# The convolution's edge columns: copied by VectorE beside its taps, and by POOL once per block; the first block's normalisation in two halves

## The chip, the cores and the metric

The kernel runs on one core of a Trainium2 chip. The core has five engines that work side by side, each on its own queue and in that queue's order: TensorE (PE in the profile) multiplies matrices, VectorE (DVE), ScalarE (ACT) and GpSimd (POOL) work on elements, and SyncE (SP) issues transfers. They wait for one another through semaphores. The metric is the time of one execution on the device in microseconds.

## The reference

The program is two layers on 2 sequences of 4,096 tokens with 512 channels, all in float32. What follows is the part that matters here, the first layer's opening:

```python
xn = _layernorm(x, axis=-1)
x1 = xn @ w1_w.T + w1_b
x_conv = _silu(_depthwise_conv(x1, conv_w))   # 3 taps along the sequence, zeros beyond its ends
v = _silu(xn @ v1_w.T + v1_b)
x_ssm = _ssm(x_conv, A, B_ssm, C_ssm, D_ssm)  # a linear recurrence over the sequence
attn = x_ssm * v @ w2_w.T + w2_b
ffn  = quantised(xn) @ quantised(weight).T + bias   # a six-bit grid, one scale to 32 elements
x = x + attn + ffn
```

The second layer (linear attention with 16 heads, and a gated feed-forward part) takes this x. Depthwise convolution means that each channel is filtered by itself: output t of a channel is w0·x1[t−1] + w1·x1[t] + w2·x1[t+1].

## The kernel before

The 8,192 tokens are cut into 16 blocks (NK) of 512 tokens (T), eight to a sequence (NB); 512 channels make four groups (CC) of 128. The kernel has stages one after another: the first, from the start to 472.7 us, is the one that the change is in. The later ones are the recurrence, the mixing with the quantised product, and the second layer. Within a stage a scheduler orders the instructions of each engine by the order of the program and its own estimates; what is written first is not always issued first.

The first stage loops over the blocks n. One turn of it does this:

- `projected(n)` (line 339) has TensorE make eight products of 128 channels by 512 tokens, each from four matrix multiplications (line 154). The first four, with the weight w1, give x1, the convolution's input; the other four, with v1, give v. Products go to four PSUM banks in turn (`acc`), so a product has to wait until the bank that was used four products earlier has been emptied. ScalarE empties them: line 351 adds the bias and writes x1, line 366 takes the silu and writes v, which a transfer sends to memory (line 367).
- The block's x1 is a tile of 514 columns for each channel group: column 0 is the last token of the block before, columns 1 to 512 are its own tokens, and column 513 is the first token of the next block. After each group's eviction `halo` (line 329) fills the edges. On POOL it copies column 512 of the block before into column 0 (line 334), and the own first token, column 1, into column 513 of the block before (line 335). At the ends of a sequence it writes zeros (lines 332 and 337).
- `tapped(n − 1, o)` (line 394) filters channel group o of the block before, which is now complete: tap 0 on ScalarE (line 397, columns 0 to 511), taps 1 and 2 on VectorE (line 399, columns from 1 and from 2). The silu on ScalarE (line 406), the transposition on VectorE (line 408) and the transfer cd on SP (line 409) are held back until the next group's eviction has been written down, by the list `tapping`.
- `turned(n + 1)` (line 320) prepares the next block's input, xnT, with channels on the partitions: sixteen rescalings of 128x128 on ScalarE (line 128) and four transpositions on VectorE (line 324). It needs each token's scale and bias.
- `measured` (line 293) makes these for two blocks at a time, in every second turn: bn_stats and bn_aggr on VectorE (lines 123 and 124), then `rstd` (line 105), a chain of small operations: VectorE (line 108), a square root on ScalarE (line 110), and VectorE again (lines 112 to 116, and 140 for the bias). `spread_out` moves the numbers through memory to another layout (SP, lines 132 and 134).
- Beside this, single tiles are quantised for the later product (ScalarE line 128, VectorE lines 176 to 193 and 389, POOL lines 180 and 194; the same for the weight with line 376), loaded on SP (xq, line 381), and the tables of the recurrence are made (VectorE lines 221 to 266, POOL lines 216, 232, 241).

SP issues, in its own order, the loads of x for the statistics (line 290), of the inputs to be turned (xi, line 317) and of xq, and the stores cd. A transfer that waits for its data holds back all transfers behind it.

The first block is different, because nothing can be loaded ahead of it. `first_turned` (line 299) waits for the statistics of all four tiles of 128 tokens, scales the four tiles on VectorE (line 304), and TensorE transposes them against the identity (line 148), with copies out of PSUM on ScalarE (line 149). The statistics of all four tiles come from one call of `measured(0, ...)`.

ScalarE computes silu and square root from different tables; where it goes from one to the other, the profile shows an ACT_TABLE_LOAD of 1.28 us under the line that needs it.

Of the kernel before, what the change touches and what calls it, by code (L numbers as in the profile page):

```python
# [10 lines left out]
F32 = mybir.dt.float32  # L11
I32 = mybir.dt.int32
AF = mybir.ActivationFunctionType
ALU = mybir.AluOpType
# [29 lines left out]
def block_kernel(ctx: ExitStack, tc: tile.TileContext, a: dict, out: bass.AP):  # L44
# [57 lines left out]
    def window(ap, steps):  # L102
        return bass.AP(tensor=ap.tensor, offset=ap.offset, ap=[list(ap.ap[0])] + steps)

    def rstd(out_ap, var_ap, n):

        v = small.tile([P, n], F32, tag="rs_v", name="rs_v")
        nc.vector.tensor_scalar(v, var_ap, EPS_LN, None, ALU.add)  # L108
        s = small.tile([P, n], F32, tag="rs_s", name="rs_s")
        nc.scalar.activation(s, v, AF.Sqrt)  # L110
        r = small.tile([P, n], F32, tag="rs_r", name="rs_r")
        nc.vector.reciprocal(r, s)
        e = small.tile([P, n], F32, tag="rs_e", name="rs_e")
        nc.vector.tensor_tensor(e, v, r, ALU.mult)
        nc.vector.scalar_tensor_tensor(e, e, -0.5, r, ALU.mult, ALU.mult)
        nc.vector.scalar_tensor_tensor(out_ap, e, 1.5, r, ALU.add, ALU.mult)

    def layernorm_stats(xt, mv):

        n = mv.shape[1]  # L120
        st = small.tile([P, n, 6], F32, tag="st", name="st")
        for j in range(n):
            nc.vector.bn_stats(st[:, j, :], xt(j))
            nc.vector.bn_aggr(mv[:, j, :], st[:, j, :])
        rstd(mv[:, :, 1], mv[:, :, 1], n)

    def rescaled(dst, src, mv):
        nc.scalar.activation(dst, src, AF.Identity, bias=mv[:, 0:1], scale=mv[:, 1:2])  # L128
# [9 lines left out]
    def as_scale_and_bias(mv):  # L138

        nc.vector.scalar_tensor_tensor(  # L140
            mv[:, :, 0], mv[:, :, 0], -1.0, mv[:, :, 1], ALU.mult, ALU.mult
        )
# [150 lines left out]
    def measured(n, xts):  # L293

        mv = mv0[:, n : n + len(xts) // TJ].rearrange("p n j k -> p (n j) k")
        layernorm_stats(lambda j: xts[j], mv)
        as_scale_and_bias(mv)

    def first_turned(work, xts):

        xnT = work.tile([P, CC, T], F32, tag="xnT", name="xnT")
        xn = work.tile([P, TJ, D], F32, tag="xi", name="xn")
        for j in range(TJ):
            nc.vector.tensor_scalar(
                xn[:, j, :], xts[j], mv0[:, 0, j, 1:2], mv0[:, 0, j, 0:1], ALU.mult, ALU.add
            )
        for j in range(TJ):
            transposed(xnT[:, :, j * P : (j + 1) * P], xn[:, j, :], ("tr", "mm")[j % 2])
        return xnT
# [16 lines left out]
            )  # L326
        return xnT

    def halo(n, o, x1, before):

        if n % NB == 0:
            nc.gpsimd.memset(x1[:, o, 0:1], 0.0)
        else:
            nc.gpsimd.tensor_copy(x1[:, o, 0:1], before[:, o, T : T + 1])
            nc.gpsimd.tensor_copy(before[:, o, T + 1 : T + 2], x1[:, o, 1:2])  # L335
        if n % NB == NB - 1:
            nc.gpsimd.memset(x1[:, o, T + 1 : T + 2], 0.0)

    def projected(work, n, xnT, before):

        x1 = work.tile([P, CC, T + 2], F32, tag="x1", name="x1")
        tapping = []

        def finish():
# [3 lines left out]
        for o in range(CC):  # L348
            pm = acc()
            product(pm, lambda k: w1[:, k, o * P : (o + 1) * P], lambda k: xnT[:, k, :])  # L350
            nc.scalar.activation(x1[:, o, 1 : T + 1], pm, AF.Identity, bias=w1_b[:, o, :])  # L351
            halo(n, o, x1, before)

            finish()
            if n:
                tapping.append(tapped(work, n - 1, before, o))
            if n == NK - 1 and o:

                tapping.append(tapped(work, n, x1, o - 1))
# [642 lines left out]
    with tc.tile_pool(name="tab", bufs=1) as tab:  # L1002
# [3 lines left out]
        with pool("a", 2) as work, pool("pm", 1) as pm:  # L1006
# [5 lines left out]
            v1 = load_weight("v1_w")  # L1012
            v1_b, conv_w = column("v1_b"), column("conv_w", 3)
            xi = laid(work, 1)
            measured(0, xts[0])
            xnT = first_turned(work, xts.pop(0))
            xts[1] = fetched(work, 1)
            measured(1, xts.pop(1))
# [190 lines left out]
```

## Time and profile before

| what | value |
| --- | --- |
| time, median of 3 runs | 2396.13 us (2393.2 to 2397.08) |
| the profiled execution: time | 2395.06 us |
| the profiled execution: span | 2393.3 us |
| TensorE busy | 2356.1 us, 98% |
| VectorE busy | 1530.0 us, 64% |
| ScalarE busy | 1013.0 us, 42% |
| POOL busy | 478.0 us, 20% |
| first product of the first stage | at 14.01 us |
| end of the first stage's products | at 472.7 us |
| 56 copies at line 335, duration | median 186 ns, up to 1179 ns |

The span is the time from the first to the last instruction that the profiler saw; the execution's own time is 1.8 us longer. A row of a timeline gives the start of a group of instructions, its length, engine, line, operation, the tile written and the tiles read, and how many they were; in square brackets stands how long the engine had been idle, and which instruction ended that idle time. A row of the waits gives the waiting instruction, the one it waited for, the sum in us, how many times, and the longest. A row of a table by stretches gives the busy time of each engine in that stretch, the granted clock of TensorE as a share of the full one (PEclk), the share of the transfer engines, and the rate of transfers.

### The profile page before, as it was taken

The page shows a single profiled execution, that of the slowest core. Times are in us where ns is not written, and L with a number is a line of the kernel's source. Part 1 is how long each engine was busy: PE and PEld are TensorE (multiplying, and loading weights), DVE is VectorE, ACT ScalarE, POOL GpSimd, SP SyncE. Part 2 cuts the span into 40 slices and gives each one's busy share as a digit, 9 for nine tenths or more (in the row PEclk, how much of TensorE's full clock was granted, in tenths as well). Part 3 has the DMA queues.
Part 4 walks back from the last instruction along what each step waited for, and adds up shares of the span by engine and source line. Part 5 has one row for each costly group of instructions (what it writes and reads, how often), then busy time and mean ns, then how long its engine had stood idle before and what let it go on. Part 6 is the DMA issues. An engine that isn't in the chain of part 4 may idle for free.

```text
span 2393.3 us, 21964 instructions
## 1 busy us (share of the span) xinstructions
PE 2356.1 (98%) x6400; PEld 1104.6 (46%) x6400; DVE 1530.0 (64%) x3050; ACT 1013.0 (42%) x1929; POOL 478.0 (20%) x534
## 2 busy tenths in 40 slices
PE   8999999999999999999999999999999999999999
PEld 3433444466444444444444555444444444445554
DVE  6888764554576654267769778666552265557777
ACT  5875674344233333146663222233333236652222
POOL 0121210122243332100102112233332100001111
PEclk9999999999999999999999999999999999999999
DMA  7854432467833342212265445433432212264331
GB/s 255 304 131 141 140 141 92 138 208 273 304 115 110 114 120 84 66 35 97 93 228 185 144 138 195 157 110 115 120 106 75 62 39 81 93 215 141 129 132 57
DMA packets 253832, 328.12 MB, mean 137 GB/s; under 512 B 55952, under 2 KB 117392, under 8 KB 252688
## 3 DMA queue, kind: packets, MB, share of 16 engines
q1 hardware_dynamic: 224624, 259.59, 34.2%
q10 hardware_dynamic: 29088, 67.12, 7.2%
q8 instruction: 51, 0.84, 0.2%
q14 instruction: 69, 0.57, 0.1%
HBM read 205.38 MB, written 121.27 MB: 136 GB/s over the span
## 4 chain that ended last, share of the span: by engine, by line
PE 67%; DVE 4%; DMA 1%; ACT 1%; issue 1%; POOL 1%; SPq 0%; POOLq 0%; ACTq 0%; DVEq 0%
PE p_acc L154 18%; PE p_tr L154 9%; PE p_acc L698 8%; PE p_mm L667 7%; PE p_mm L652 7%; PE p_mm L823 6%; PE p_acc L823 6%; PE p_tr L823 2%; PE p_mm L950 1%; PE p_tr L950 1%; PE p_acc L652 1%; PE p_tr L652 1%; PE p_acc L667 1%; PE p_acc L488 0%; DVE t L886 0%
## 5 line engine op out<-in xcount | busy, mean ns | idle before, releaser
L154 PE MATMUL p_acc<-xnT,w_v_w 128*128 128x512 f32 x512 | 227.8, 600 | 10.3 <-ACT x L351 10.3
L698 PE MATMUL p_acc<-k,x 128*128 128x512 f32 x512 | 229.9, 592 | 0.9 <-ACT k L733 0.9
L154 PE MATMUL p_acc<-xnT,w_w_w 128*128 128x512 f32 x512 | 223.1, 593 | 2.7 <-DVE xnT L324 1.1
L154 PE MATMUL p_acc<-w_W_v,t 128*128 128x512 f32 x512 | 222.3, 592 | 0.0
L154 PE MATMUL p_acc<-w_W_r,xnT 128*128 128x512 f32 x448 | 201.4, 592 | 0.0
L154 PE MATMUL p_tr<-w_Wk,xnT 128*128 128x512 f32 x448 | 199.2, 592 | 0.1
L971 POOL TENSOR_TENSOR x<-x,row_beta 128x512 f32<-128x512 f32 x64 | 83.8, 1310 | 552.8 <-ACT xn L128 547.4
L667 PE MATMUL p_mm<-w_w_w,t 128*128 128x512 f32 x416 | 186.7, 592 | 0.0
L652 PE MATMUL p_mm<-w_d,t 128*128 128x512 f32 x384 | 173.6, 593 | 1.4 <-DVE x L675 1.2
L110 ACT ACTIVATE rs_s<-rs_v 128x4 f32<-128x4 f32 (+1 forms) x41 | 8.3, 205 | 391.5 <-DVE rs_v L108 391.5
L154 PEld LDWEIGHTS p_acc<-xnT,w_v_w 128*128 128x128 f32 x512 | 97.7, 192 | 137.9 <-issue 115.0
L696 POOL TENSOR_TENSOR ksum<-ksum,k 128x512 f32<-128x512 f32 x62 | 83.4, 1344 | 368.8 <-ACT k L733 368.8
L154 PEld LDWEIGHTS p_acc<-xnT,w_w_w 128*128 128x128 f32 x512 | 96.8, 190 | 126.8 <-issue 117.0
L698 PEld LDWEIGHTS p_acc<-k,x 128*128 128x128 f32 x512 | 97.2, 190 | 123.7 <-issue 120.8
L154 PEld LDWEIGHTS p_acc<-w_W_v,t 128*128 128x128 f32 x512 | 97.3, 190 | 122.5 <-issue 119.1
L732 DVE TENSOR_TENSOR k<-p_tr,row_bk 128x512 f32<-128x512 f32 x64 | 43.8, 684 | 162.1 <-PE p_tr L154 162.1
L977 ACT ACTIVATE r<-p_acc 128x512 f32<-128x512 f32 x64 | 38.2, 597 | 249.8 <-PE p_acc L154 237.5
L399 DVE SCALAR_TENSOR_TENSOR xc<-x,col_conv_w,xc 128x512 f32<-128x512 f32 x128 | 95.7, 763 | 63.1 <-POOL x L335 30.9
L154 PEld LDWEIGHTS p_tr<-w_Wk,xnT 128*128 128x128 f32 x448 | 85.0, 190 | 107.6 <-issue 104.0
L180 POOL TENSOR_TENSOR xq<-xq,mx_rs 128x512 f32<-128x512 f32 x64 | 76.4, 1194 | 269.8 <-DVE mx_rs L179 188.6
L733 ACT ACTIVATE k<-k 128x512 f32<-128x512 f32 x64 | 40.1, 627 | 203.4 <-DVE k L732 194.8
L667 PEld LDWEIGHTS p_mm<-w_w_w,t 128*128 128x128 f32 x416 | 79.0, 190 | 99.5 <-issue 99.5
(223 smaller groups left out, 4054.4 us busy)
## 6 DMA issues: line engine op xcount, KB each, us to landing
x<-in_x SPq DMA_DIRECT2D x126, 256.0 KB, 3.5
xq<-in_xi SPq DMA_DIRECT2D x64, 256.0 KB, 4.5
vd<-v ACTq DMA_DIRECT2D x64, 256.0 KB, 2.3
cd<-xs SPq DMA_DIRECT2D x64, 256.0 KB, 2.0
xg<-cd SPq DMA_DIRECT2D x16, 1024.0 KB, 6.7
v<-vd SPq DMA_DIRECT2D x64, 256.0 KB, 4.8
xd<-x SPq DMA_DIRECT2D x64, 256.0 KB, 2.0
qd<-q ACTq DMA_DIRECT2D x64, 256.0 KB, 2.0
```

The costliest lines, as they stand in the source:

```text
L154: nc.tensor.matmul(out_ap, lhsT=lhsT(k), rhs=rhs(k), start=(k == 0), stop=(k == CC - 1))
L180: nc.gpsimd.tensor_tensor(by_block(y), by_block(y), rs.unsqueeze(2).to_broadcast([P, NQ, QB]), ALU.mult)
L399: nc.vector.scalar_tensor_tensor(xc, x1[:, cc, tap : tap + T], conv_w[:, cc, tap : tap + 1], xc, ALU.mult, ALU.add,)
L652: nc.tensor.matmul(po, lhsT=xds[i][j][:, k, :], rhs=wd[:, k, :], start=(k == 0), stop=False)
L667: nc.tensor.matmul(po, lhsT=z[:, k, j * P : (j + 1) * P], rhs=w2[:, k, :], start=False, stop=(k == CC - 1),)
L696: nc.gpsimd.tensor_tensor(ksum, ksum, kt, ALU.add)
L698: nc.tensor.matmul(pg[c], lhsT=xn[:, c * P : (c + 1) * P], rhs=kt, start=first, stop=last)
L732: nc.vector.tensor_tensor(kt, pk, bk, ALU.add)
L733: nc.scalar.activation(kt, kt, AF.Relu)
L823: nc.tensor.matmul(banks[c], lhsT=lhsT(k, c), rhs=rhs(k), start=first and k == 0, stop=k == 1, skip_group_check=True,)
L950: nc.tensor.matmul(pc[:, c, :], lhsT=qT[:, 2 * c2 + c, tj], rhs=kvx[:, 2 * c2 + c, :], start=True, stop=True,)
L971: nc.gpsimd.tensor_tensor(xt[j], xt[j], beta, ALU.add)
```

## The change

The edges of the convolution are filled in another way. `halo` is gone. `from_last`, called once at the start of a block, copies column 0 of all four groups in one POOL instruction (128x4) from the block before, or writes zeros. `to_last`, called after each group's eviction where `halo` was, copies the own first column into column 513 of the block before, on VectorE instead of POOL. The zeros at a sequence's end are written for four groups at once.

The first block's statistics and scaling are done by halves, two tiles of 128 tokens each: `first_turned` itself calls `layernorm_stats` for the first two tiles and scales them on ScalarE (`rescaled`), then for the other two and scales these on VectorE as before. The second half's statistics use the place of the first half's scratch tile, which `rstd` and `layernorm_stats` now take as arguments.

```diff
@@ -102,7 +102,7 @@
     def window(ap, steps):
         return bass.AP(tensor=ap.tensor, offset=ap.offset, ap=[list(ap.ap[0])] + steps)
 
-    def rstd(out_ap, var_ap, n):
+    def rstd(out_ap, var_ap, n, e=None):
 
         v = small.tile([P, n], F32, tag="rs_v", name="rs_v")
         nc.vector.tensor_scalar(v, var_ap, EPS_LN, None, ALU.add)
@@ -110,19 +110,21 @@
         nc.scalar.activation(s, v, AF.Sqrt)
         r = small.tile([P, n], F32, tag="rs_r", name="rs_r")
         nc.vector.reciprocal(r, s)
-        e = small.tile([P, n], F32, tag="rs_e", name="rs_e")
+        if e is None:
+            e = small.tile([P, n], F32, tag="rs_e", name="rs_e")
         nc.vector.tensor_tensor(e, v, r, ALU.mult)
         nc.vector.scalar_tensor_tensor(e, e, -0.5, r, ALU.mult, ALU.mult)
         nc.vector.scalar_tensor_tensor(out_ap, e, 1.5, r, ALU.add, ALU.mult)
 
-    def layernorm_stats(xt, mv):
+    def layernorm_stats(xt, mv, st=None, e=None):
 
         n = mv.shape[1]
-        st = small.tile([P, n, 6], F32, tag="st", name="st")
+        if st is None:
+            st = small.tile([P, n, 6], F32, tag="st", name="st")
         for j in range(n):
             nc.vector.bn_stats(st[:, j, :], xt(j))
             nc.vector.bn_aggr(mv[:, j, :], st[:, j, :])
-        rstd(mv[:, :, 1], mv[:, :, 1], n)
+        rstd(mv[:, :, 1], mv[:, :, 1], n, e)
 
     def rescaled(dst, src, mv):
         nc.scalar.activation(dst, src, AF.Identity, bias=mv[:, 0:1], scale=mv[:, 1:2])
@@ -300,10 +302,24 @@
 
         xnT = work.tile([P, CC, T], F32, tag="xnT", name="xnT")
         xn = work.tile([P, TJ, D], F32, tag="xi", name="xn")
-        for j in range(TJ):
-            nc.vector.tensor_scalar(
-                xn[:, j, :], xts[j], mv0[:, 0, j, 1:2], mv0[:, 0, j, 0:1], ALU.mult, ALU.add
-            )
+        for half in range(2):
+            js = range(2 * half, 2 * half + 2)
+            mv = mv0[:, 0, 2 * half : 2 * half + 2]
+
+            if half:
+                layernorm_stats(lambda j: xts[2 + j], mv, st=place)
+            else:
+                place = small.tile([P, 2, 6], F32, tag="st", name="st")
+                layernorm_stats(lambda j: xts[j], mv, e=place[:, 0, 0:2])
+            as_scale_and_bias(mv)
+            for j in js:
+                if half:
+                    nc.vector.tensor_scalar(
+                        xn[:, j, :], xts[j], mv0[:, 0, j, 1:2], mv0[:, 0, j, 0:1],
+                        ALU.mult, ALU.add,
+                    )
+                else:
+                    rescaled(xn[:, j, :], xts[j], mv0[:, 0, j, :])
         for j in range(TJ):
             transposed(xnT[:, :, j * P : (j + 1) * P], xn[:, j, :], ("tr", "mm")[j % 2])
         return xnT
@@ -326,19 +342,23 @@
             )
         return xnT
 
-    def halo(n, o, x1, before):
-
+
+    def from_last(n, x1, before):
         if n % NB == 0:
-            nc.gpsimd.memset(x1[:, o, 0:1], 0.0)
+            nc.gpsimd.memset(x1[:, :, 0:1], 0.0)
         else:
-            nc.gpsimd.tensor_copy(x1[:, o, 0:1], before[:, o, T : T + 1])
-            nc.gpsimd.tensor_copy(before[:, o, T + 1 : T + 2], x1[:, o, 1:2])
+            nc.gpsimd.tensor_copy(x1[:, :, 0:1], before[:, :, T : T + 1])
         if n % NB == NB - 1:
-            nc.gpsimd.memset(x1[:, o, T + 1 : T + 2], 0.0)
+            nc.gpsimd.memset(x1[:, :, T + 1 : T + 2], 0.0)
+
+    def to_last(n, o, x1, before):
+        if n % NB:
+            nc.vector.tensor_copy(before[:, o, T + 1 : T + 2], x1[:, o, 1:2])
 
     def projected(work, n, xnT, before):
 
         x1 = work.tile([P, CC, T + 2], F32, tag="x1", name="x1")
+        from_last(n, x1, before)
         tapping = []
 
         def finish():
@@ -349,7 +369,7 @@
             pm = acc()
             product(pm, lambda k: w1[:, k, o * P : (o + 1) * P], lambda k: xnT[:, k, :])
             nc.scalar.activation(x1[:, o, 1 : T + 1], pm, AF.Identity, bias=w1_b[:, o, :])
-            halo(n, o, x1, before)
+            to_last(n, o, x1, before)
 
             finish()
             if n:
@@ -1012,7 +1032,6 @@
             v1 = load_weight("v1_w")
             v1_b, conv_w = column("v1_b"), column("conv_w", 3)
             xi = laid(work, 1)
-            measured(0, xts[0])
             xnT = first_turned(work, xts.pop(0))
             xts[1] = fetched(work, 1)
             measured(1, xts.pop(1))
```

## The prediction

> **What bounds the kernel now.** I read the page's busy line first, then TensorE's waits, then stretches of the first stage, then the timeline around the longest stall.
>
> ```profile
> PE 2356.1 (98%) x6400; PEld 1104.6 (46%) x6400; DVE 1530.0 (64%) x3050; ACT 1013.0 (42%) x1929; POOL 478.0 (20%) x534
> ```
> ```profile
> PE p_acc L154 <- ACT x L351: 10.3, 8, 3.4
> PE p_tr L148 <- DVE xn L304: 9.7, 1, 9.7
> ...
> PE p_acc L154 <- DVE xnT L324: 1.1, 1, 1.1
> ```
> ```profile
> core 0: us, PE busy (x) PEld busy (x) DVE busy (x) ACT busy (x) POOL busy (x), PEclk, DMA share, GB/s
> ...
> 156.30:181.00 24.70, 21.13 (x48) 8.95 (x48) 20.00 (x33) 17.89 (x39) 9.36 (x5) 0.99 0.44 94
> 181.00:187.50 6.50, 6.31 (x8) 2.70 (x9) 6.50 (x8) 6.25 (x10) 0.18 (x1) 0.51 0.37 113
> ...
> 335.30:472.70 137.40, 137.39 (x320) 60.91 (x321) 68.76 (x89) 68.26 (x120) 9.69 (x41) 1.00 0.33 114
> ```
> ```profile
> 175.94 1.88 PE L154 MATMUL p_acc<-xnT,w_v_w 128*128 128x512 f32 x4
> 181.19 6.33 PE L154 MATMUL p_acc<-xnT,w_v_w 128*128 128x512 f32 x7 [3.37 <-ACT x L351]
> ```
> ```profile
> 174.00 3.62 DVE L237 TENSOR_TENSOR kf<-kf,col_D_ssm 128x4 f32<-128x4 f32 x1
> ...
> 178.80 0.74 DVE L399 SCALAR_TENSOR_TENSOR xc<-x,col_conv_w,xc 128x512 f32<-128x512 f32 x1
> ```
> ```profile
> 179.57 0.63 ACT L406 ACTIVATE xc<-xc 128x512 f32<-128x512 f32 x1 [4.82 <-DVE xc L399]
> 180.11 0.44 ACT L240 COPY kr<-kf 128x32 f32<-128x32 f32 x3
> 180.46 0.68 ACT L351 ACTIVATE x<-p_acc,col_w_b 128x512 f32<-128x512 f32 x1
> ```
>
> TensorE is busy 98% of the span, so only its own waits can be won, and the change touches only the first stage, 14.0 to 472.7 us. A block there that waits for nothing takes 27.47 us, measured over blocks 11 to 15 (137.4 / 5, give or take their edges). Sixteen make 439.5 of 458.7 us: 19.2 us are lost, and 14.0 us pass before the first product. The waits say who is late: ScalarE empties a bank (L351) too late. Its queue is in order, and a silu (L406) ahead of the eviction waits for VectorE's tap (L399). At 174 us that tap stands behind L237, four columns, which takes 3.62 us while POOL's L241 runs from 173.51 to 177.59. The eviction starts at 180.46, TensorE idles 3.37 us, and then runs at a granted 0.51 for 6.5 us: another 3.2 us. Two shorter waits in block 6 (1.84 and 2.10 us, behind evictions at 209.67 and 215.47) left the clock at 1.00. The rest: 1.06 us at block 1, 1.42 in block 3, 0.44 in block 4, 0.80 before block 5's long gap, 1.16 in block 10.
>
> **The change part by part.** The profiled execution took 2395.06 us, a span of 2393.3; it is 1.07 under the median of 2396.13. The sum is made against 2395.06.
>
> *Column copies.* Off POOL go 56 copies L334 and 56 L335 (median 186 ns for L335) and 16 memsets of about 98 ns; on come 14 copies of 128x4 and 4 memsets: some 17 us of POOL queue fall away. POOL is 20% busy, so by itself that is worth nothing. VectorE gets 56 copies of one column. No such copy is in the trace: above, L217's copy of 64 columns, 194 ns (10.9 us in all); below, the 0.07 us by which small operations follow one another at 110.02, 110.09 and 110.18 us (3.9 us in all). I take 0.1, 5.6 us, since these copies stand in a full queue like the latter. Blocks 11 to 15 (VectorE 50% busy there) and block 7 to 9 hide theirs; without that cover they cost the whole 5.6. The 20 of blocks 2 to 6 fall where VectorE is busy 84.4 of 95 us (128 to 223): 2.0 us, within 1.4 to 3.9.
>
> What VectorE gains is the wait at L399 for POOL's L335: 30.9 us in 13 waits, but 14.3 of it is one wait in the last block and most others are in blocks where TensorE sets the pace. Only 0.50 us at 319.49 in block 10 stands ahead of a late eviction, where L335 queued on POOL behind row_w_b (L1089): gain 0.5, up to 1.2 if the following waits of that block vanish with it, 0 if ScalarE is late anyway. The eviction L351 loses its wait for POOL's reads and the tap 0 (L397) gets a wait for the new block copy. That copy waits for the last eviction of the block before, ready a whole half block earlier, and for taps of two blocks back; behind it on POOL are only quantisation's L180 and L194.
>
> [...]
>
> *Order.* The order of instructions before and after differs far more than the edit: within the first stage VectorE, ScalarE, POOL and SP are reshuffled, TensorE and all later stages are not. What I find in it:
> - Block 1: the statistics' multiplier (L108) comes behind more work, and the last two of sixteen rescalings L128 behind the last silu v(0,3), which TensorE releases at 41.7. The last transposition L324 then ends near 44.0 instead of 42.8: +1.2 us (0 to 1.5, by L366 0.69, two L128 0.86, L324 0.68). Blocks 3 to 6 wait for ScalarE by the clock and swallow this; it is charged as 0 in the sum.
> - Block 2: on SP the load xq is issued after the third cd, at about 91.2, not after the fourth at 94.46. ScalarE waited 3.31 us for that load at 100.33 with sixteen rescalings behind. Gain 3.3 for the chain of ScalarE and VectorE, 0 if SP's x loads (14 ahead, up to 12.47 us) take it back.
> - Block 5: the same L237 stands behind the same L241 and costs 3.62 again; between L237 and the tap at 178.80 an L192 (0.60 to the next) and two small operations replace L188 and L176: equal within 0.2. Block 5's fourth eviction (186.25) now stands ahead of a table load (1.28) and a silu, and on the way to block 6 L376 (0.71, after 0.26 of waiting) is put off: gain 0.8 there.
>
> So the evictions of blocks 5 and 6 come 3.3 − 2.0 + 0.8 = 2.1 us earlier on one count; adding the waits of L115 and L188 behind POOL at 199.32 and 200.34 (1.01 and 1.25 us instead of the usual 0.17 and 0.41), of which the order after may spare one, I get 2.9. I take 2.9, within −4.8 (all of it, and the copies at 1.4) and +1.5 (no xq gain, and the copies at 3.9 less the 0.8, half of it swallowed by VectorE's idle 10.6 us).
>
> What is late next is block 6. TensorE now reaches it with block 3 and 4's 1.86 and most of block 5's 3.37 + 3.2 in hand, while the evictions it needs are only 2.9 earlier: its first wait grows from 1.84 to about 5 us. By the nearest row, 3.37 us of idle gave half clock and 2.10 did not, so I charge the half clock there again: 3.2 at most, less the 2.10 of the second wait, that the slower products fill: +1.1. Sum: start 0, blocks 1 to 6 −2.9 + 1.1 = −1.8, block 10 −0.8 (between 0.5 and 1.2), later 0: −2.6, 2392.5; a further −0.5 for evictions freed of POOL's wait in block 4 and 6 (between 0 and 1), 2392.0.
>
> [...]
>
> *First block's halves.* TensorE waits 9.7 us for xn (L304), begins at 9.69 and turns a tile each 0.86 us; the first product starts at 14.01. The first half's L108 comes at about 6.65 instead of 7.42, after three L123 instead of four; 0.44 to L112 and 0.97 for the small chain (7.86 to 8.99, less the mask's reductions between) give 8.06. But its two scalings go to ScalarE at 0.80 us each (the 128x512 form of L128; 0.70 with the usual overlap), and the second half's square root stands behind them, at 9.46; with 0.24 to L112, 0.97 again and 0.54 for L304 the third tile is ready near 11.2, and TensorE turned it at 11.42. Within −0.5 (all four earlier) and +0.5: taken as 0.
>
> **Rivals.**
> 1. *Large gain:* no half clock anywhere, and the chain 4.8 earlier: −4.8, block 10 −1.2, evictions −1, start −0.5, and of block 1 to 4's waits 1 more: 8.5, 2386.6. For it: the earlier xq. Against: L237 still waits for L241. All 19.2 gone would be 2375.9.
> 2. *Nothing:* the wait for POOL becomes one for ScalarE, and the x loads on SP take back the xq: 2395, within 1.5.
> 3. *Slower:* VectorE is nearly full to 223 us; the 20 added copies at 0.19 (3.8 us), with no xq gain and 0.8 spared, push the evictions of blocks 5 and 6 back by 3.0, and both first gaps pass 3.37 us, so a second half clock of 3.2 follows: +6.2, 2401.3. It decides from the point where the copies cost more than the xq brings: at 0.19 us each with a gain under 1.4. Against: the 0.07 spacing.
>
> **How the numbers follow.** Forecast (−2 to −6 counts as one case) 38%, large gain 27%, nothing 12%, slower 23%. A measurement of this kernel tells about 0.2%, 4.8 us, from no change: faster is under 2391.3, slower over 2400.9. Of the forecast case 14 fall under 2391.3 and 24 between; with the large gain 41% faster; with "nothing" 36% the same; 23% slower. The range 2383 to 2402 leaves out the far end of the large gain and of slower, some 8 and 10%. The predicted time is 2392.0; the forecast case's own range is 2389 to 2394.
>
> **What would show it.** Right: the gap at block 5's third eviction under 2 us at full clock, block 6's first gap over 3.4 us with a clock near 0.5 behind it; xq's wait at 100 us gone; first product at 14.0 ± 0.5; VectorE's copies spaced by about 0.1; block 1 begins near 44. Wrong: a copy that holds VectorE 0.2 us or more, block 5's gap as before or longer, the first product over 0.5 earlier or later, or a changed stretch after 472.7 us less its start.

## The result: slower by 0.28%

The changed kernel takes 2403.33 us (median of 7 runs, 2402.14 to 2406.6), the kernel before 2397.35 (median of 7, 2393.2 to 2399.69). The ratio is 1.0028, with a 95% interval of 1.0016 to 1.0040: slower by more than the 0.2% that can be told from no change, and above the predicted range. The profiled execution after took 2402.45 us, its span is 2400.7, which is 7.4 more than before's 2393.3.

The page's busy line of the kernel after:

```profile
PE 2359.0 (98%) x6400; PEld 1106.2 (46%) x6400; DVE 1536.9 (64%) x3110; ACT 1013.6 (42%) x1932; POOL 457.8 (19%) x424
```

POOL has lost 20.2 us of work, VectorE has gained 6.9. TensorE's own work has grown by 2.9 us with the same 6400 matmuls: some of them ran slower (block 1's first 32, below, took 16.81 us instead of 14.00). TensorE's waits after, each with the sum, the times and the longest:

```profile
PE p_acc L156 <- ACT x L371: 10.7, 5, 4.6
PE p_tr L150 <- ACT xn L130: 9.1, 1, 9.1
PE p_acc L156 <- DVE mv L126: 6.3, 1, 6.3
```

The waits for evictions (L371, before L351) are as long in sum as before, in five pieces instead of eight. The third row is new, one wait of 6.3 us. Timeline of TensorE after, three stretches:

```profile
47.66 16.81 PE L156 MATMUL p_acc<-xnT,w_w_w 128*128 128x512 f32 x32 [6.28 <-DVE mv L126]
...
188.43 9.54 PE L156 MATMUL p_acc<-xnT,w_v_w 128*128 128x512 f32 x16 [4.55 <-ACT x L371]
...
219.00 13.04 PE L156 MATMUL p_acc<-xnT,w_v_w 128*128 128x512 f32 x24 [3.87 <-ACT x L371]
```

The new wait is at the start of block 1, and the 32 matmuls behind it take 16.81 us where before they took 14.00:

```profile
42.80 14.00 PE L154 MATMUL p_acc<-xnT,w_w_w 128*128 128x512 f32 x32 [1.06 <-DVE xnT L324]
```

Blocks 5 and 6 wait 4.55 and 3.87 us, before 3.37 and 1.84 (with a second wait of 2.10 in block 6). Three stretches after, block 5, block 6 and blocks 11 to 15:

```profile
162.70:197.80 35.10, 30.50 (x66) 12.94 (x65) 29.09 (x42) 25.19 (x50) 9.74 (x5) 0.90 0.38 95
197.80:231.90 34.10, 30.23 (x66) 12.94 (x65) 29.93 (x56) 16.81 (x33) 7.45 (x8) 0.90 0.36 114
342.80:480.20 137.40, 137.40 (x322) 60.84 (x321) 70.92 (x109) 67.62 (x120) 3.37 (x6) 1.00 0.33 116
```

The granted clock falls to a mean of 0.90 in both blocks now; before, block 6 kept its clock (1.00 from 191.22 to 223.40). The last five blocks take 137.40 us as before. The first stage's products end at 480.16 us instead of 472.74: these 7.42 us are the whole difference, and the later stages are unchanged.

The clearest view of where time goes is the start of each block's first product, read off TensorE's timeline. The table has these starts as us later than in the kernel before (whose own starts stand in the second column); the other columns are kernels of the experiments below.

| block | before, at | after | halves_only | halves_turn | conv_ordered | last_dve | last_dve2 | late_tables |
| --- | --- | --- | --- | --- | --- | --- | --- | --- |
| 0 | 14.01 | −0.37 | 0.24 | 0.08 | −0.17 | 0.06 | 0.06 | −0.27 |
| 1 | 42.80 | 4.86 | 6.01 | 0.70 | 1.48 | 4.11 | 1.50 | 0.69 |
| 2 | 70.37 | 7.67 | 7.56 | 1.99 | 1.48 | 4.11 | 1.49 | 2.38 |
| 4 | 127.55 | 5.44 | 5.48 | 4.21 | 0.34 | 4.11 | 4.35 | 0.14 |
| 5 | 156.30 | 6.39 | 9.12 | 6.05 | 1.29 | 5.05 | 5.83 | 0.36 |
| 6 | 191.22 | 6.58 | 9.41 | 5.01 | 1.04 | 4.67 | 6.71 | −6.52 |
| 7 | 223.40 | 8.48 | 8.03 | 4.66 | 3.00 | 6.33 | 9.47 | −4.18 |
| 9 | 278.44 | 8.37 | 8.03 | 4.66 | 3.00 | 6.33 | 9.47 | −0.90 |
| 10 | 305.90 | 8.38 | 8.36 | 4.67 | 6.75 | 7.90 | 12.84 | −0.89 |
| 11 | 335.31 | 7.51 | 8.22 | 3.23 | 7.05 | 8.63 | 13.29 | −2.84 |

Down the column "after": −0.37 at the start, +5.23 ahead of block 1, +2.81 in block 1 (slow matmuls), −2.23 in block 3, whose short waits are gone because TensorE comes later, +1.14 in blocks 4 and 5, +1.90 in block 6, −0.1 to block 10, −0.87 in block 10. The prediction had put the loss at block 1 at 1.2 and had let it be swallowed.

One caution for reading single profiles: the part up to block 1 differs by 2 to 4 us between executions of the same instructions (see the last section), so a column is to be read from its block 1 or 2 on, and totals from the timed runs.

**What happens ahead of block 1.** VectorE's timeline after, the end of block 1's turn:

```profile
38.77 0.69 DVE L125 BATCH_NORM_STATS2 st<-x 128x6 f32<-128x512 f32 x1 [2.41 <-DMA x<-in_x]
...
43.82 0.68 DVE L340 STREAM_TRANSPOSE xnT<-xi 128x512 f32<-128x512 f32 x1
44.43 1.25 DVE L125 BATCH_NORM_STATS2 st<-x 128x6 f32<-128x512 f32 x2
45.59 0.17 DVE L126 BATCH_NORM_AGGREGATE mv<-st 128x2 f32<-128x6 f32 x1
45.67 0.66 DVE L125 BATCH_NORM_STATS2 st<-x 128x6 f32<-128x512 f32 x1
46.24 0.17 DVE L126 BATCH_NORM_AGGREGATE mv<-st 128x2 f32<-128x6 f32 x1
46.33 0.66 DVE L125 BATCH_NORM_STATS2 st<-x 128x6 f32<-128x512 f32 x1
46.90 0.70 DVE L340 STREAM_TRANSPOSE xnT<-xi 128x512 f32<-128x512 f32 x1
```

and ScalarE's last rescaling for it:

```profile
43.42 0.49 ACT L130 ACTIVATE xi<-xi,mvi 128x128 f32<-128x128 f32 x1 [0.93 <-DMA x<-in_x]
```

The last of block 1's four transpositions needs only this rescaling, done at 43.91. It starts at 46.90, because four bn_stats of later blocks, with their aggregations, stand ahead of it: 2.5 us. (The row of TensorE's wait names L126, which ended just before TensorE started; the input that it lacked is this transposition, which ends at 47.60.) Right behind the rescaling the transposition would have ended at some 44.6 us, an estimate from its own 0.7 us. So of the 4.86 us by which block 1 starts later, 1.9 are ScalarE's, whose last rescaling comes later, and 3.0 are the order of VectorE's queue. The bn_stats that waits 2.41 us for its load of x is not new: before, one waited 2.47 us in the same place, between the first two transpositions. In VectorE's order 16, 19, 21 and 25 bn_stats precede the four transpositions; before it was 15, 17, 20 and 22. The diff does not touch these lines; the scheduler put them so when the first block's statistics became two smaller sets. TensorE's clock after this wait, in steps of 2 us:

```profile
47.66:49.66 2.00, 2.00 (x3) 0.97 (x4) 2.00 (x10) 0.21 (x1) 0.00 (x0) 0.50 0.41 142
49.66:51.66 2.00, 2.00 (x4) 0.87 (x3) 2.00 (x12) 0.00 (x0) 0.26 (x1) 0.50 1.03 365
51.66:53.66 2.00, 2.00 (x4) 0.76 (x3) 0.73 (x2) 0.00 (x0) 0.79 (x1) 0.58 0.68 195
53.66:55.66 2.00, 2.00 (x6) 0.87 (x5) 0.73 (x4) 1.44 (x2) 0.00 (x0) 1.00 0.49 171
```

It is granted 0.50 for some 5.7 us behind 6.28 us of idling. The view counts 3 or 4 matmuls that touch a stretch of 2 us at half clock, and 6 in the one at full clock.

### The profile page after: what moved, and what is told of

Same layout as the page of the kernel before. It is cut to its first block, busy times and chain, and to the rows that moved or that the text cites. A ratio compares the mean times of both kernels' runs of the same rounds, so it can differ in the third digit from the quotient of the medians.

```text
span 2400.7 us, 21882 instructions
## 1 busy us (share of the span) xinstructions
PE 2359.0 (98%) x6400; PEld 1106.2 (46%) x6400; DVE 1536.9 (64%) x3110; ACT 1013.6 (42%) x1932; POOL 457.8 (19%) x424
## 4 chain that ended last, share of the span: by engine, by line
PE 69%; DVE 4%; ACT 1%; issue 1%; DMA 1%; POOL 1%; SPq 0%; POOLq 0%; ACTq 0%; DVEq 0%
PE p_acc L156 18%; PE p_tr L156 9%; PE p_acc L718 9%; PE p_mm L687 7%; PE p_mm L672 7%; PE p_mm L843 6%; PE p_acc L843 6%; PE p_tr L843 2%; PE p_mm L970 1%; PE p_tr L970 1%; PE p_acc L672 1%; PE p_acc L508 1%; PE p_acc L687 1%; PE p_acc L518 1%; PE p_tr L672 1%
## 5 line engine op out<-in xcount | busy, mean ns | idle before, releaser
L110 ACT ACTIVATE rs_s<-rs_v 128x4 f32<-128x4 f32 (+2 forms) x42 | 8.5, 205 | 391.8 <-DVE rs_v L108 391.8
L130 ACT ACTIVATE xq<-xq,mvi 128x128 f32<-128x128 f32 x256 | 104.7, 480 | 38.6 <-DMA xq<-in_xi 35.3
```

## The experiments

Two theories stood at the start: the delay at block 1, that is, the place that the scheduler gave statistics and transpositions (called A in the expectations), and the copies on VectorE's queue (B). A third came with the second set: not the edit's work but the reshuffled order of everything else. Ratios below are to the kernel before, timed beside each set, with 95% intervals.

### Each half of the change alone

conv_only has the edges copied as in the change (block copy on POOL, last column on VectorE) and the first block as before. halves_only has the first block by halves, and `halo` as before.

> The kernel before with the column copies of the change alone; the first block as before. Theory A (the halves reorder block 1, and that is the whole loss): the four transpositions of block 1 stand behind 15, 17, 20 and 22 bn_stats as in the kernel before, block 1 begins at 42.8 +- 0.5, and the time is that of before, 2397, within 4 us. Theory B (the 56 copies on VectorE push the evictions of blocks 5 and 6 back): the time is 5 to 7 us over before, with the first product at 14.0 and block 1 at 42.8, and the loss comes after 97 us.

> The kernel before with the first block by halves alone; the edge columns by POOL as before. Theory A: the transpositions of block 1 stand behind 16, 19, 21 and 25 bn_stats, as with the whole change; block 1 begins near 47.7 after an idle TensorE of some 6 us and at half clock, and the time is 5 to 9 us over before. Theory B: the time is that of before within 3 us, since the delay of block 1 is taken up by the waits of blocks 3 to 6.

Measured: conv_only 2402.5, 1.0022 (1.0013 to 1.0031); halves_only 2404.38, 1.0030 (1.0019 to 1.0042). Each part alone costs what the whole does, and the two do not add. In halves_only TensorE waits at the same place, and the same four bn_stats stand ahead of the last transposition:

```profile
48.81 15.55 PE L156 MATMUL p_acc<-xnT,w_w_w 128*128 128x512 f32 x32 [5.06 <-DVE mv L126]
```

conv_only has the bn_stats as before (15, 17, 20, 22) and no such wait. So there are two causes.

### The place of block 1 in the queues

Two edits of the whole change. stats_after holds the statistics of blocks 4 and 5 behind block 1's last transposition; turn_first lets the whole of block 1's turn go ahead of other work.

```diff
-                    xnT = turned(work, n + 1, xi)
+                    if n == 0:
+                        with tc.high_priority():
+                            xnT = turned(work, n + 1, xi)
+                    else:
+                        xnT = turned(work, n + 1, xi)
...
+                if n == 2:
+                    with tc.issue_after(turned_1[0]):
+                        measured(n + 2, xts.pop(n + 2) + xts.pop(n + 3))
```

(The first five lines are turn_first, the last three stats_after.)

> The whole change, with the statistics of blocks 4 and 5 put behind the last transposition of block 1 in VectorE's order, and nothing else asked for. Theory A (the queue on VectorE is what makes block 1 late): the last transposition follows ScalarE's last rescaling (43.9 with the whole change) at once, block 1 begins at 44.5 or earlier, a gap of 3 us instead of 6.3, without half clock; the time is 5 to 7 us below the whole change's 2403.3. Rival (the rescalings on ScalarE and their late scale and bias are what makes it late): block 1 begins within 1 us of 47.7 and the time stays above 2401.

> The whole change, with all of block 1's sixteen rescalings and four transpositions ahead of the rest, on ScalarE ahead of the silus of v and on VectorE ahead of the statistics of blocks 4 and 5. Theory A: sixteen rescalings from 29.6 at 0.39 us end near 36, the last transposition near 37, so TensorE goes from block 0 to block 1 without a gap at about 41.4; the time is 7 to 10 us below the whole change, 2394 to 2396. Rival (the loss lies in the copies and comes back in blocks 5 and 6): block 1 begins at 41.4, but the time stays above 2400.

Measured: stats_after 2403.59, 1.0032 (1.0021 to 1.0043); turn_first 2398.82, 1.0004 (0.9996 to 1.0013). In stats_after block 1's wait falls to 2.42 us, as meant, but block 4 then waits 4.39 us for an eviction, with slow matmuls behind it (10 in 7.26 us, where before 10 took 4.46), and nothing is won: A's forecast of the total failed there. In turn_first block 1 starts at 43.38 without a wait, the four transpositions having 16, 16, 16 and 17 bn_stats ahead, and the ratio falls from the whole change's 1.0028 to 1.0004. That is between the two forecasts, 2394 to 2396 and over 2400, so A's forecast of the total was too low here as well.

halves_turn is the same edit on halves_only:

> The halves alone (edge columns on POOL as before), in the scheduler's order but with block 1's rescalings and transpositions first. If the 7.5 us of the halves-alone run are block 1's place in the queues: 5 us or more below it, within 3 us of before. If the halves cost elsewhere too: above 2400.5.

Measured: 2397.07, 0.9995 (0.9986 to 1.0004), against 1.0030 without the edit. So all that the halves cost is block 1's place in the queues: with it mended they cost nothing.

### Work or order

For these the first stage's instructions are held, on each engine's queue, in the order of another kernel. The edit is a list of positions for each engine, and an order edge without a semaphore from each instruction to the next:

```diff
+        for e, order in ORDER.items():
+            for i, j in zip(order, order[1:]):
+                tc.add_manual_dep(
+                    lists[e][j], lists[e][i].name,
+                    mybir.DependencyInfo(mybir.DependencyClass.NoSync, mybir.DependencyReason.DATA),
+                    reason="order",
+                )
```

conv_ordered, halves_ordered and both_ordered have the work of conv_only, of halves_only and of the whole change in the order of the kernel before (what is new stands beside what it replaces); before_reshuffled has the work of before in the order of conv_only on VectorE, ScalarE and SP; POOL, with all its copies, is left to the scheduler. In the three ordered kernels each copy on VectorE stands directly ahead of the tap that reads it.

> The column copies of the change alone, but with the first stage's instructions held in the kernel before's order on VectorE, ScalarE, SP and POOL; each of the 56 copies stands just ahead of the tap 2 that reads it. Order theory (the copies cost next to nothing, the new order costs the 5.6 us of the copies-alone run): the time is that of before, 2397, within 2.5 us, block 1 begins at 42.8 but for the clock of the first products. Copy theory (VectorE's copies lengthen the chain): the time is 4 to 7 us over before.

> The halves alone, in the kernel before's order but for the first block's own statistics and scaling. Order theory: block 1 begins at about 42.8, not 48, and the time is that of before within 2.5 us, perhaps 0.3 less for a first product at 13.7 to 14.3. Rival (the statistics of block 1 themselves come later, whatever the order): block 1 begins after 45 and the time is 4 us or more over before.

> The whole change in the kernel before's order. Order theory: within 3 us of before, so 5 to 8 us under the whole change as the scheduler orders it; a gain over before of 0.5 to 1.5 us could come from block 10's wait for POOL. Rival: over 2401.

> The kernel before with not one instruction changed, but with VectorE, ScalarE and SP in the first stage held in the order that the scheduler gives the copies-alone kernel (56 copies left out of it; POOL still makes its 112). Order theory: slower than before by 4 to 7 us, as the copies-alone kernel is. Copy theory: the time of before within 2.5 us.

| kernel | median us | ratio (95%) |
| --- | --- | --- |
| conv_ordered | 2403.69 | 1.0028 (1.0017 to 1.0040) |
| halves_ordered | 2397.77 | 1.0001 (0.9992 to 1.0010) |
| both_ordered | 2404.08 | 1.0025 (1.0015 to 1.0035) |
| before_reshuffled | 2397.72 | 1.0002 (0.9994 to 1.0011) |

For the copies the order theory falls: they cost 0.28% in the old order, and the new order without them costs nothing. For the halves it holds: in the old order they are free.

The profiles of conv_only and before_reshuffled, the same order with and without the copies, say where the copies cost. From block 2 to block 7 both fall back alike, by 1.81 and 1.70 us; in blocks 9 and 10 conv_only loses 3.70 us and the other gains 1.06. About 1.6 of that is half clock behind a wait of 2.56 us in block 10 (16 matmuls in 8.75 us instead of 7.13); whether that wait is all the copies' own was not shown. These are single profiles.

### The copies themselves

Three kernels in the order of before (first_block with POOL left to the scheduler). last_dve moves only the 56 copies of L335 from POOL to VectorE, last_dve2 does each of these twice, and first_block has only the block copy of column 0, on POOL.

```diff
-            nc.gpsimd.tensor_copy(before[:, o, T + 1 : T + 2], x1[:, o, 1:2])
+            nc.vector.tensor_copy(before[:, o, T + 1 : T + 2], x1[:, o, 1:2])
+            nc.vector.tensor_copy(before[:, o, T + 1 : T + 2], x1[:, o, 1:2])
...
-            nc.gpsimd.tensor_copy(x1[:, o, 0:1], before[:, o, T : T + 1])
+            nc.gpsimd.tensor_copy(x1[:, :, 0:1], before[:, :, T : T + 1])
```

(Three lines of last_dve2, of which last_dve has the first two; then first_block.)

> The kernel before in its own order, with only the 56 copies of line 335 moved from POOL to VectorE, each just ahead of its tap 2; column 0 is still copied per group by POOL. If VectorE's copies are the cost (0.18 us of queue each, seen at 210.76 and 210.94 in the ordered copies): 3 to 6 us over before. If the block copy on POOL is the cost (it waits for the last eviction with the quantisation's L180 behind it): within 2 us of before.

> The same with every VectorE copy made twice (112 copies). If VectorE's copies are the cost: about twice the excess of the single ones, 6 to 11 us over before. If they are not: as the single ones, within 2 us.

> The kernel before with only column 0 copied for four groups at once (14 POOL copies of 128x4 and 4 memsets instead of 72 small operations); line 335 stays on POOL; VectorE, ScalarE and SP in the order of before, POOL as the scheduler has it. If VectorE's copies are the cost: within 2.5 us of before. If the block copy is the cost: 3 to 6 us over before.

Measured: last_dve 2402.95, 1.0020 (1.0011 to 1.0029); last_dve2 2407.36, 1.0043 (1.0031 to 1.0056); first_block 2396.53, 0.9998 (0.9988 to 1.0007). The medians lie 5.7, 10.1 and −0.7 us from the 2397.26 beside them (by the ratios 4.8, 10.3 and −0.5): the cost grows with the number of copies, and the block copy is free.

The timeline shows the price of one. VectorE in last_dve, block 9:

```profile
301.71 0.14 DVE L335 COPY x<-x 128x1 f32<-128x1 f32 x1
301.88 0.75 DVE L399 SCALAR_TENSOR_TENSOR xc<-x,col_conv_w,xc 128x512 f32<-128x512 f32 x1
```

and the same place in last_dve2:

```profile
306.27 0.14 DVE L335 COPY x<-x 128x1 f32<-128x1 f32 x1
306.44 0.15 DVE L336 COPY x<-x 128x1 f32<-128x1 f32 x1
306.63 0.75 DVE L400 SCALAR_TENSOR_TENSOR xc<-x,col_conv_w,xc 128x512 f32<-128x512 f32 x1
```

The next instruction starts 0.17 to 0.19 us behind each copy; over last_dve's 56 copies the median is 0.18, and the sum 10.1 us. That is the price of a copy directly ahead of its tap. In the kernel after, the scheduler puts many copies elsewhere, as here in block 3:

```profile
122.98 0.13 DVE L356 COPY x<-x 128x1 f32<-128x1 f32 x1
123.04 1.03 DVE L428 STREAM_TRANSPOSE xs<-xc 128x512 f32<-128x512 f32 x1
```

There the next instruction starts 0.12 us or less behind 22 of the 56, 15 of them among the 20 of blocks 2 to 6, and those 20 steps add up to 2.2 us. The copies themselves last as long, a median of 146 ns.

Behind the tap stand its silu on ScalarE and the next eviction. The evictions of block 9 start, on ScalarE's timeline, at

| kernel | four evictions of block 9 | steps |
| --- | --- | --- |
| before | 287.27, 292.61, 296.62, 300.91 | 5.34, 4.01, 4.29 |
| last_dve | 294.49, 299.82, 303.98, 308.44 | 5.33, 4.16, 4.46 |
| last_dve2 | 299.06, 304.38, 308.72, 313.38 | 5.32, 4.34, 4.66 |

The last two steps grow by 0.15 and 0.17 with one copy, by 0.33 and 0.37 with two: here each copy passes undiminished to the bank that TensorE waits for. Block 9 by stretches, before, last_dve and last_dve2 in turn (the third number is TensorE's busy time, then its weight loads, then VectorE's):

```profile
278.44:305.90 27.46, 27.46 (x65) 12.16 (x64) 27.01 (x43) 15.56 (x32) 12.10 (x16) 1.00 0.32 112
```
```profile
284.77:313.80 29.03, 27.89 (x65) 11.88 (x63) 28.53 (x47) 15.22 (x32) 10.81 (x13) 1.00 0.29 110
```
```profile
287.91:318.74 30.83, 28.29 (x66) 11.72 (x64) 29.90 (x56) 15.92 (x33) 11.53 (x14) 1.00 0.30 111
```

Before, VectorE is busy 27.01 of block 9's 27.46 us. The block is full to the edge, and grows with the copies: by 1.57 and 3.37 us. Four copies at 0.18 would be 0.7 of the 1.57. Another 0.89 us is there when the block begins: TensorE starts block 9 6.33 us later than before, as it did block 7, but its first eviction comes 7.22 later. What TensorE had not felt in blocks 7 and 8 stayed in VectorE's queue. Read from block 2 on in the table above, last_dve loses 2.22 us up to block 7 and 2.30 in blocks 9 and 10, and last_dve2 7.98 and 3.82.

### What takes the load off VectorE

If VectorE's chain is the limit, taking other work out of blocks 6 to 11 should gain. late_tables is the kernel before with the recurrence's tables (L216 to L266) made in blocks 11 to 15 instead.

```diff
-                if n in (6, 7, 9):
-                    next(powers)
-                if 8 <= n < 8 + CC:
-                    chunk_tables(*made, n - 8)
+                if n == 11:
+                    with tc.issue_after(last_turn[0].ins):
+                        for _ in range(3):
+                            next(powers)
+                if 12 <= n < 12 + CC:
+                    with tc.issue_after(last_turn[0].ins):
+                        chunk_tables(*made, n - 12)
```

> The kernel before, with the recurrence's tables (L216 to L266: the powers, the sums of 3.7 and 3.6 us, the transpositions of 1.9 us, some 27 us of VectorE) made in blocks 11 to 15, where TensorE sets the pace, not in blocks 2 to 6. If VectorE's queue ahead of the evictions is what makes blocks 3 to 6 late: the waits of 3.4, 1.8 and 2.1 us and the half clock shrink to under 3 us together, and the time is 6 to 12 us below before, 2386 to 2391. If the lateness has another source: within 3 us of before, or slower if blocks 12 to 15 now wait.

Measured: 2393.03, 0.9984 (0.9975 to 0.9992). It is faster than the kernel before by 4.2 us, by 3.8 by the ratio, and so the fastest kernel of this study, but the gain was forecast at 6 to 12 us, and the waits of 2.77 and 2.00 us below are more than the 3 us together that the forecast left. TensorE in block 6:

```profile
184.70 14.00 PE L154 MATMUL p_acc<-xnT,w_w_w 128*128 128x512 f32 x32 [0.30 <-ACT v L368]
...
204.90 8.77 PE L154 MATMUL p_acc<-xnT,w_v_w 128*128 128x512 f32 x16 [2.77 <-ACT x L353]
215.68 3.70 PE L154 MATMUL p_acc<-xnT,w_v_w 128*128 128x512 f32 x8 [2.00 <-ACT x L353]
```

Block 5's long wait and its half clock are gone (the table's 0.36 turns to −6.52 by block 6). Most of that is given back in blocks 6 and 7, where TensorE again waits for evictions (−0.90 at block 9); block 10, now without its tables, brings it to −2.84. The order here is the scheduler's new one, so what the move of the tables is worth by itself, and what the new order, was not told apart.

late_copies puts the 56 copies on VectorE into late_tables, in its order; late_best adds to late_tables the block copy on POOL and turn_first's edit.

> The kernel with the tables made late, in its own order, with the 56 copies of line 335 on VectorE ahead of their taps. If a copy costs because VectorE's queue sets the pace in blocks 3 to 6 and 9 to 10, and the freed queue takes it up: within 2.5 us of the late tables without it, 2393 to 2395.5, and under the kernel before. If a copy costs wherever it stands (it lengthens the step from one engine to the other): 4 to 6 us over the late tables, 2397 to 2399.

> The late tables, with column 0 by block on POOL (line 335 on POOL too), the first block whole as before, and block 1's rescalings and transpositions first. If the three add up: the 4 us of the late tables and another 1 to 2 us for block 1's gap of 1.1 to 2.0, so 2391 to 2392. If block 1's gap is taken up by the later waits: 2393, as the late tables alone.

Measured: late_copies 2397.1, 0.9993 (0.9984 to 1.0002); late_best 2400.13, 1.0007 (0.9998 to 1.0016). With VectorE relieved the copies cost 0.09% (by the medians, each against its own set, 3.4 us), less than the 0.20% in the old order, but the intervals overlap; in the trace its evictions still fall behind late_tables', by 1.9 us at block 6 (197.26 to 195.36) and by 4.3 at block 9 (285.48 to 281.18). That is inconclusive. late_best is a plain miss: the late tables, which gained, are slower together with the block copy, which costs nothing alone, and with turn_first's edit, which was not run alone on the kernel before. Its trace has waits of 2.68, 1.21 and 1.40 us in block 7, where those of late_tables are 0.54 at most. Every such edit is a new order of four queues; why this one is worse was not settled.

## Why the prediction was wrong

- **Block 1** is the step that failed, and the largest in this trace: "+1.2 us (0 to 1.5 …) … charged as 0". It was 4.86 us (5.23 more of waiting, for a start 0.37 earlier), with 2.81 of half clock behind it, for which the sum had no term. The working priced what stands behind the statistics' multiplier and on ScalarE, which came to 1.9 us, and passed over the four bn_stats that VectorE's order has between the third and the fourth transposition (3.0 us with what stands around them). The order of VectorE's queue showed them. "Blocks 3 to 6 wait for ScalarE by the clock and swallow this" was right in kind and small: 2.23 us in block 3. turn_first, an edit of block 1's place only, takes the ratio from 1.0028 to 1.0004.
- **Where the copies cost** was the second: 2.0 us for the 20 copies of blocks 2 to 6, and "Blocks 11 to 15 … and block 7 to 9 hide theirs." For blocks 11 to 15 this holds (137.40 us as before). For block 9 it does not: VectorE was busy 27.01 of 27.46 us there, in a stretch that the prediction did not look at, and what blocks 7 and 8 hide comes out there. In last_dve the copies alone cost about 5 us, half of it in blocks 9 and 10. In the kernel after, with TensorE 8.4 us late, these two blocks cost nothing.
- **The price of a copy**, 0.1 us, bounded by 0.07 and 0.194, depends on what stands behind it. Directly ahead of its tap it is 0.18, near the row for L217; among other small operations it is 0.12 or less, like the rows at 110.02 that the prediction went by. For the kernel after, with 2.2 us in blocks 2 to 6, the sum's 2.0 was about right.
- **The load xq** came as predicted: ScalarE's wait of 3.31 us for it at 100.33 is gone. In the first stage these waits were 10.6 us in three, the longest, 6.4, in block 9; they are after, with the 4.4 in block 9:

```profile
ACT xq L130 <- DMA xq<-in_xi: 4.9, 2, 4.4
```

  The evictions fit that: those of block 2 start up to 8.1 us later than before (97.17 to 89.06), the last of block 3 only 4.6 (127.85 to 123.29). But by block 5's first it is 7.3 again (175.90 to 168.62). The steps behind the five copies in between are 0.6 of these 2.7 us; the rest was not told apart. So the "2.9 earlier" that the sum gave the evictions of blocks 5 and 6 did not come: they are 5.5 to 8.7 us later than before.
- **L237 behind L241** was priced at 3.62 us again. After, it takes 0.15 us (as L239), and it is the tap itself that lasts 4.13 us, while POOL's L243 (before, L241) runs from 180.61 to 184.42:

```profile
180.45 0.14 DVE L356 COPY x<-x 128x1 f32<-128x1 f32 x1
180.51 0.42 DVE L190 TENSOR_SCALAR c<-xq 128x512 int32<-128x512 int32 x1
180.84 4.13 DVE L419 SCALAR_TENSOR_TENSOR xc<-x,col_conv_w,xc 128x512 f32<-128x512 f32 x1
184.89 0.15 DVE L239 TENSOR_TENSOR kf<-kf,col_D_ssm 128x4 f32<-128x4 f32 x1
```

  The price stayed, on another instruction. The gap at block 5's third eviction, to be "under 2 us at full clock", was 4.55 with a half clock.
- **Right** were: POOL's relief worth nothing; nothing changed behind the first stage; the start within ±0.5 (−0.37: the first transposition at 9.09, not 9.69), though profiles of kernels with the first block whole start their products from 13.68 to 14.16 as well.
- **Right by luck** were two. Block 6's first wait was over 3.4 us (3.87) with a half clock, 2.47 us where 3.2 at most was charged (13.04 for 24 matmuls instead of 10.57). But TensorE was to come earlier, and the evictions less so; in fact TensorE comes 6.58 us later and the eviction 8.60 (218.27 to 209.67). Block 10's gain was 0.87, the 0.8 of the sum, but not shown to be the wait for POOL: with the edges still on POOL before_reshuffled gains 1.06 there and halves_turn 1.44, and last_dve, without that wait, loses 0.73.
- **A bound** of the sum does not come out: "−4.8 (all of it, and the copies at 1.4)" is 3.3 − 1.4 + 0.8 + 2 × 0.84 = 4.4. The rival with the large gain used it too: with 4.4 its 2386.6 would be 2387.0.
- **The rivals.** The slower one, copies at 0.19 us that push the evictions of blocks 5 and 6 back and bring a second half clock, gave 2401.3 and a chance of 23%. Its mechanism is what conv_ordered, last_dve and last_dve2 show, though in blocks 9 and 10 as much as in 5 and 6. It held the xq gain as what decides; that gain came and did not decide. In the kernel after, most of the loss is at block 1, which this rival does not have, so its 2401.3 lies near the measured time for another reason. The copies' turning the wait for POOL into one for ScalarE, rival 2, is seen in VectorE's waits after, in place of 30.9 us in 13 waits for L335:

```profile
DVE x L356 <- ACT x L371: 30.2, 14, 13.9
```

**Why the two costs do not add** is only partly shown. By the runs, the copies cost 0.28% in the order of before and 0.24% on top of halves_ordered, 0.09% on top of halves_turn (within the noise: turn_first, with all 56 copies, has 0.9996 to 1.0013), and nothing on top of halves_only. So their cost depends on the order around them. TensorE that comes 5 us late at block 1 and 7.7 at block 2 meets banks that have had longer to be emptied, which fits: in block 9 TensorE is 8.37 us later than before and the four evictions 4.27 to 7.05, in conv_only 4.80 and 3.27 to 6.05. But after and halves_only have also different orders from block 4 on (6.39 and 9.12 us late at block 5, 8.48 and 8.03 at block 7), so what the copies would cost in the same order with a late block 1 was not measured.

## What to carry to other kernels

Each one-column copy put on VectorE's queue cost a whole step of it: some 0.18 us directly ahead of the tap that reads it, 0.12 or less ahead of many other instructions. Whether an engine can hide it is read block by block, not from its share of the span (64% and yet 98% in block 9), and what one block hides can come out in the next, as 0.89 us did at the start of last_dve's block 9. Where a scheduler orders the queues, compare the order of every engine around each point where the bound engine starts a new block, and count what stands between its last inputs: the longest new wait of this change, 6.28 us, came from lines that the diff does not touch. To price work apart from order, run the new work in the old order and the old work in the new one.

## What was not expected of the hardware

The start of the first stage is not the same from execution to execution. In profiles of the kernels before and after, and of conv_ordered, both_ordered, before_reshuffled, first_block, late_tables and late_copies, the first 32 matmuls take 14.0 us; in the nine others 15.5 to 16.3, though the instructions up to there are in several of them the same. First before, then last_dve:

```profile
14.01 14.00 PE L154 MATMUL p_acc<-xnT,w_w_w 128*128 128x512 f32 x32 [0.68 <-ACT xnT L149]
```
```profile
14.07 16.33 PE L154 MATMUL p_acc<-xnT,w_w_w 128*128 128x512 f32 x32 [0.68 <-ACT xnT L149]
```

The extra time lies at the start: in stretches of 2 us from the first product on, the views count 3, 4, 5 and 6 matmuls in last_dve, and 5, 6 and 6 in before. They print a granted clock of 1.00 in all of these, but they print it also where the trace has no clock record, as from 9 to 11 us of before, whose record begins at 13.30, with the full clock (after's at 12.39). That last_dve ran at half clock at first is an estimate from these counts: its 32 matmuls took 2.33 us more, as some 4.7 us at half clock would give. Block 1's wait varied as well where VectorE's order up to it was the same: 1.06 us in before, 2.77 in last_dve, 0.74 in last_dve2, where bn_stats wait for loads of x. A single profile can so be 2 to 4 us off with nothing changed up to there, most of what this study is about; only the timed runs could tell.

Half clock came behind shorter waits than 3.37 us, and not always. Waits of 2.02 us (late_tables, at 43.49), 2.12 (halves_turn, 191.00), 2.57 (halves_ordered, 211.78) and 2.68 (late_best, 236.68) were followed by it, the first by 32 matmuls in 15.70 us instead of 14.00, the last three by 8 in 5.4 us instead of 3.7; waits of 2.63 (first_block, 208.64), 2.97 (late_copies, 44.39) and 3.44 (halves_only, 200.63) were not: the matmuls behind them ran at full pace, 8 in 3.70 us or 32 in 14.00.

The clock records of before and after show where the granted clock was half ahead of the last matmul: once in before, from 180.56 us, and three times in after, from 46.53, 186.47 and 217.19, for 6.83 us each. From the record's beginning on, the full clock ahead of these stretches lasted 167.25 us in before, and 34.13, 133.12 and 23.89 in after. All of these are whole multiples of 3.41 us: 49, then 10, 39 and 7, and 6.83 is two. In the 3.41 us just ahead of half clock TensorE idled 2.73 us in before, and 3.41, 2.60 and 2.06 in after. Cut at the same step, no other piece at full clock held more than 1.84 us of idle time in either; the wait of 1.84 us in before's block 6, which kept its clock, is one of these. In these two traces the length of the wait sorts them as well, 3.37 us or more against 2.10 or less; what sorts the waits of the other kernels above was not shown.
